# Post-LN attention with routed experts: half of the down weights kept on the chip, and the last batch's row gathers split in two

## The chip, the cores and the metric

The kernel runs on one core of a Trainium2 chip. The metric is the device time of one launch in microseconds (us); lower is better. Before and after compute the same function with the same inputs and outputs. Engines are called as the profile calls them: PE is TensorE (matmuls), PEld its weight loads, DVE is VectorE, ACT is ScalarE, POOL is GpSimd (here above all the issuer of the indirect row gathers), and SP is the queue that issues nearly all other DMAs.

## The reference

The input is `x` of shape (4, 512, 256): four batches of 512 tokens, 256 features.

```python
x = layernorm(x + attention(x))          # 16 heads of 16, causal, ALiBi bias
x = layernorm(x + ffn(x))

def ffn(h):                              # 64 experts, top 8, plus one shared expert
    logits = h @ gate_w.T
    topv, topi = top_k(logits, 8)
    W = scatter(topi, softmax(topv))
    inter = silu(gate_e(h)) * up_e(h)    # each expert e: 256 -> 64
    out = sum_e (inter_e * W[:, e]) @ down_e     # 64 -> 256
    return out + sigmoid(h @ sh_gate1) * shared_expert(h)
```

## The kernel before

All four batches go through two stages that overlap. The first stage is attention, output projection, layer norm and routing. The second is the expert part, and it fills most of the second half of the run.

**Expert part.** The 64 experts of a batch are taken in 16 steps of four (`QUAD`), counted q = 0 to 15; a step of batch b is written b.q below. Each expert has 30 slots (`CELL`) for each 128-token tile, so a step handles up to 120 slots by four experts.

- `gather()` (L995) uses PE to pull the chosen tokens of 16 experts (a group, four steps) into a tile `xt`. It does a group in eight half pieces, each of six short matmuls (L1020), which ACT and DVE copy out of PSUM (L1010).
- `up()` (L1034) first asks for the down weights of the step: a tile `dq` of 128x512 values (256 KB), loaded on SP (L1038), in a ring of four. Then it does 32 matmuls (L1049) and applies the activation, one instruction on ACT (L1057) and two on DVE (L1058, L1059).
- `down()` (L1074) multiplies by `dq` in eight matmuls (L1081). ACT copies the result out of PSUM (L1093), and SP stores it to the DRAM table `rows_out[b]` (L1094), in the order of steps: row = (q, slot, expert).
- `fetch()` (L1156) brings rows back for each tile t of 128 tokens and each of its eight chosen experts k: one indirect DMA on POOL (L1160), 128 rows of 256, into a ring of eight buffers `got` (`RING`). So a batch needs 4 x 8 = 32 gathers, and all four need 128.
- `combine()` (L1167) multiplies the gathered rows by their weight and adds them to `xs[b]` on DVE (L1171). After the last k of certain tiles it runs the second layer norm and stores the output.

**Which rows a gather may need.** Within a token the eight row numbers are sorted, the greatest first. Therefore k = 4 to 7 are the lower four of eight, and where a batch is handled in two halves their gathers are given a table slice that leaves out the last step. Batches 0 to 2 do this: first all (t, k = 4 to 7), then all (t, k = 0 to 3), and row numbers of the first half are clamped below the last step (L876 to L878).

**The last batch.** `LATE = (0, 0, 0, 4)`: the last four steps of batch 3 (3.12 to 3.15) never go through DRAM. Their results stay in SBUF (L1088), weights are spread over the slots by DMA and DVE (`spread_in()` L1102, `weigh()` L1113), and `collect()` (L1125) adds them by 128 matmuls into PSUM (L1135) and four additions of 128x256 (L1143). So for batch 3 the table's last step is 3.11. Before the change this batch is not done in two halves: its 32 gathers go tile by tile, and each may read the whole table, step 3.11 included.

**What sets the order.** Every function above is a generator, and `ORDER` (L37) is a string with one letter for each resumption: p, s, v, o, r for the first stage, h, g, u, d for the expert steps, i for a gather, c for a combine, w, e, k for the late steps, z for the final range check. The string is played once while the program is built, so each engine receives its instructions in that order and runs its own queue strictly in it. In the region that matters later, before the change PE has: all of group 3.3 (steps 3.12 to 3.15) mixed with ups 3.8 and 3.9; then down 3.7, down 3.8, up 3.10, up 3.11, down 3.9, down 3.10, up 3.12, down 3.11, down 3.12, up 3.13 to 3.15 and the collects. The first gather of batch 3 is queued on POOL after the gathers of batch 2.

**Attention's buffers.** In `context()` (L740) a 128x512 tile `avs` with two buffers holds sums on their way to DRAM (L760 to L762); in `output()` (L778) a 128x512 tile `scale`, also with two buffers, holds the normalisation that comes back (L788). `cxT`, 128x2x512, has two buffers (L743). None of them is used any more when batch 3's output projection (L808) has run.

Of the kernel before, what the change touches and what calls it, by code (L numbers as in the profile page):

```python
# [8 lines left out]
FP = mybir.dt.float32  # L9
# [3 lines left out]
ALU = mybir.AluOpType  # L13
AX = mybir.AxisListType

P = 128
HEADS, HD = 16, 16
TOP = 8
# [10 lines left out]
QUAD = 4  # L29
RING = 8  # L30
PRB = (2, 1, 1)
LATE = (0, 0, 0, 4)
# [4 lines left out]
ORDER = (  # L37
    "pppppspppspsppsvvvsppvsvsvsvsvvspsovsvpsvvvspsppopposvvsvsoovsrrrvvsvspsvvvrhrosrrsvvsvrhrsvsrsrprhh"
    "rgvvvspogspprvphphporshvrvvsoorsprrgsvvvgsroghsvrgsrvvrvsrrsvsgvvsorvsrrgvvorsvsrosorsorrrrvvsvsvvvv"
    "tuguugguuggrhglogrgdrruuugrddrruuurrdorlgguuruuggdgrougrudgogrugllrugdudduggruuggrghrhhuuhgdhhdguuuu"  # L40
    "ghddgrrhugudguudrghgriiirgdgiguggruuuiiiuugicigcduigucigdcrgdigcuucgciuugddrczcccgigciiiiricduruuigg"
    "igugrgcguuiggcdgcihhucudhcuuhicddiughuuudcihggiiciugucddgirchhuiguuugdgcgccddggicciciuuucugcgguccgud"
    "guigciiicduccddccgcguugccggguiiguicchccuudugiiidcciigiiiiguucugigdgccuuigigchcidhiucduhhiuducghdchuu"
    "cgguudchcigghcuudigcuiugdgcidccdcigicuuiggcicuiguigiuccgudugggiiucicidcdccdcccruuccgggguuiciigcuwwug"
    "gccdugidgiiicichdgiuccugccggieguccugecuiiiicdiiduuuiucciccdcduiddwciicciiicicicuuiuuucciwccicciccccc"
    "uceecckdiiidkciicdciickicicicckicicckicicicicciiiiiiicickickiiccccccccccckcccz"
)
# [362 lines left out]
def kernel(  # L410
# [23 lines left out]
    nc = tc.nc  # L434
    fast = ctx.enter_context(ExitStack())
    B, S, E = x.shape
    NT = S // P
# [302 lines left out]
    def context():  # L740

        for b in range(B):
            cxT = cxs[b] = mpool.tile([P, KC, S], FP, tag="cxT", name=f"cxT_{b}", bufs=2)  # L743
            for c, par, n in units:
# [12 lines left out]
                if n < len(blocks) - 1:  # L757
                    yield
                    continue
                avs = mpool.tile([P, S], FP, tag="avs", name=f"avs_{b}_{c}_{par}", bufs=2)  # L760
                nc.scalar.copy(avs, av)
# [16 lines left out]
    def output():  # L778

        for b in range(B):  # L780
            scales = []
            for c in range(KC):
                part = slice(HEADS // KC * c, HEADS // KC * (c + 1))
                rs = sums_in[b, c]
                rel = small.tile([P, SPAN], FP, tag="rel", name=f"rel_{b}_{c}")
                nc.vector.reciprocal(rs, rs)
                nc.sync.dma_start(out=turned[b][part].rearrange("h (j i) -> (h j) i", i=SPAN), in_=rs)
                scale = mpool.tile([P, S], FP, tag="scale", name=f"scale_{b}_{c}", bufs=2)  # L788
                for h in range(HEADS // KC):
                    nc.sync.dma_start(  # L790
                        out=scale[HD * h : HD * (h + 1), :],
                        in_=turned[b][part][h : h + 1, :].to_broadcast([HD, S]),
                    )
                scales.append(scale)
                nc.vector.tensor_tensor(rel, rs, least[:, c, :], ALU.mult)
                nc.vector.scalar_tensor_tensor(fine, rs, 1.0 / LIMIT, fine, ALU.is_ge, ALU.mult)
                nc.vector.scalar_tensor_tensor(fine, rel, LIMIT, fine, ALU.is_le, ALU.mult)
                yield
            cxT = cxs[b]
            for c in range(KC):  # L800
                nc.vector.tensor_tensor(cxT[:, c, :], cxT[:, c, :], scales[c], ALU.mult)
            yield
            xb = xs[b]
            for t in range(0, NT, 2):
                po = single(f"po_{b}_{t}").rearrange("p (t e) -> p t e", e=E)
                for u in range(2):
# [10 lines left out]
    def route():  # L817

        for b in range(B):
# [47 lines left out]
            nc.vector.scalar_tensor_tensor(row, place, float(QUAD), number, ALU.mult, ALU.add)  # L867
            nc.vector.tensor_tensor(row, row, chosen, ALU.mult)
            r8 = small.tile([P, NT, TOP], FP, tag="r8", name=f"r8_{b}")
            for t in range(NT):  # L870
# [4 lines left out]
            nc.vector.tensor_scalar(at, near, SOON[b] - 1.0, None, ALU.min)  # L875
            if not LATE[b]:  # L876
                part = slice(TOP // 2, TOP)
                nc.vector.tensor_scalar(at[:, :, part], near[:, :, part], SOON[b] - QUAD * SLOTS - 1.0, None, ALU.min)  # L878
            ats[b] = at
# [27 lines left out]
            if LATE[b]:  # L907
# [5 lines left out]
                nc.vector.reciprocal(total, total)  # L913
                nc.vector.memset(rest[:, :, FIRST[b] :], 0.0)
                yield
# [8 lines left out]
                for t in range(NT):  # L924
                    nc.tensor.transpose(pt[: 2 * EL, t * P : (t + 1) * P], pair[:, t].rearrange("p w e -> p (w e)"), ident)
                flip = rpool.tile([P, TOP, NE], FP, tag="pick", name=f"flip_{b}", bufs=2)
                flip = flip.rearrange("p k e -> p (k e)")
# [67 lines left out]
    def gather():  # L995

        for n, (b, g) in enumerate(groups):
# [7 lines left out]
            for t in range(NT):  # L1005
# [9 lines left out]
                for turn in range(2):  # L1015
# [16 lines left out]
                    yield  # L1032

    def up():  # L1034

        for n, (b, q) in enumerate(steps):
            dq = late["pool"].tile([P, QUAD // 2, E], FP, tag="dq", name=f"dq_{b}_{q}", bufs=4)
            nc.sync.dma_start(out=dq, in_=dp[:, 2 * q : 2 * q + 2, :])  # L1038
            downs[n] = dq
# [85 lines left out]
    def collect():  # L1125

        for b in range(B):
# [3 lines left out]
            for n in range(LATE[b]):  # L1131
# [8 lines left out]
                yield  # L1140
            for t in range(NT):
                part = xs[b][:, t, :]
                nc.vector.tensor_tensor(part, acc[t // 2][:, t % 2, 0:E], part, ALU.add)  # L1143
                yield
# [4 lines left out]
    for b in range(B):  # L1149
        if LATE[b]:  # L1150
            moves += [(b, t, k) for t in range(NT) for k in range(TOP)]
        else:
            moves += [(b, t, k) for t in range(NT) for k in range(HALF, TOP)]
            moves += [(b, t, k) for t in range(NT) for k in range(HALF)]

    def fetch():  # L1156

        for n, (b, t, k) in enumerate(moves):
            g = got[n] = late["pool"].tile([P, E], FP, tag="got", name=f"got_{b}_{t}_{k}", bufs=RING)
            nc.gpsimd.indirect_dma_start(  # L1160
                out=g, out_offset=None, in_=rows_out[b][0 : SOON[b] - (QUAD * SLOTS if not LATE[b] and k >= HALF else 0)],
                in_offset=bass.IndirectOffsetOnAxis(ap=ats[b][:, t, k : k + 1], axis=0),
                bounds_check=None, oob_is_err=True,
            )
            yield

    def combine():  # L1167

        for n, (b, t, k) in enumerate(moves):
# [4 lines left out]
            yield  # L1174
            last = k == (HALF - 1 if not LATE[b] else TOP - 1)
            if b < B - 1 and t % 2 and last:
# [110 lines left out]
```

## Time and profile before

| | |
|---|---|
| median of 3 timed runs | 525.33 us (525.16 to 530.65) |
| the profiled execution, its own time | 479.91 us |
| its span, first to last instruction | 477.4 us |
| mean granted PE clock in it | 0.959 |
| DMA traffic | 82.68 MB, of it 64 loads of `dq` of 256 KB and 60 stores of `rows_out` of 480 KB |
| PE busy in 300 to 400 us | 95.9 of 100 us |
| PE busy in 400 to 440 us | 31.5 of 40 us |
| PE busy in 440 to 478 us | 3.6 of 38 us |
| POOL gathers | 128, mean 980 ns each |

The profiled execution is 45.4 us shorter than the median of the timed runs. The page does not say where the timed runs spend the difference. Durations below are those of the profiled execution.

The page is read from the top: busy shares, then the 40 slices (one is about 12 us), then the chain that ended last. Attention fills the slices up to about 180 us, and then the expert part follows. The last three slices are different from all others: PE has little or nothing left, and POOL and DVE finish.

### The profile page before, as it was taken

The numbers are of one execution on the slowest core, as the hardware profiler recorded it, in microseconds if no ns is written. First come the engines' busy times: TensorE is split into PE (matmuls) and PEld (weight loads), VectorE is DVE, ScalarE is ACT, GpSimd is POOL, SyncE is SP. The second block draws the span as 40 slices with busy tenths as digits, with TensorE's granted clock in tenths as the row PEclk, the third lists the DMA queues.
The fourth block names the chain that finished last, engine by engine and source line by source line (L and its number), as shares of the span: only waits on it lengthen the run. The fifth ranks groups of instructions, "written<-read, shape, count | busy, mean of one in ns | idle before, by whom it ended". The sixth has DMA issues, their size and how long they took to land.

```text
span 477.4 us, 12454 instructions
## 1 busy us (share of the span) xinstructions
PE 423.1 (89%) x4887; PEld 284.3 (60%) x4887; DVE 339.7 (71%) x922; ACT 244.8 (51%) x454; POOL 205.6 (43%) x238
## 2 busy tenths in 40 slices
PE   8999999998999989999999999999999997878100
PEld 3535454453644556876878778777787775765100
DVE  1522326798976888986786798889778898487474
ACT  2658647773578734446646547563566545322000
POOL 6424522253324610310027664266553666457771
PEclk9999999999999999999999999999999999897855
DMA  7900110000000043886868969889899899798342
GB/s 215 405 36 5 28 25 3 24 7 24 3 25 28 8 170 99 260 284 250 240 161 280 284 210 299 267 241 305 267 283 317 255 289 325 231 278 212 105 105 74
DMA packets 37238, 82.68 MB, mean 173 GB/s; under 512 B 8276, under 2 KB 14548, under 8 KB 36148
## 3 DMA queue, kind: packets, MB, share of 16 engines
q1 hardware_dynamic: 30484, 64.51, 43.1%
q0 software_dynamic: 6144, 16.79, 12.1%
q8 instruction: 40, 0.66, 0.6%
q10 hardware_dynamic: 544, 0.52, 0.3%
q14 instruction: 26, 0.21, 0.1%
HBM read 49.88 MB, written 31.92 MB: 171 GB/s over the span
## 4 chain that ended last, share of the span: by engine, by line
PE 68%; DVE 12%; DMA 8%; ACT 4%; issue 3%; POOL 2%; SPq 1%; DVEq 0%; POOLq 0%; ACTq 0%
PE gu L1049 19%; PE y L1081 11%; PE px L1020 9%; PE sT L724 8%; PE av L752 6%; DMA got<-rows_out,at 4%; PE pv L695 3%; PE pq L678 3%; PE pk L678 3%; PE po L808 2%; DMA dq<-in_dp_dram 2%; ACT yq L1093 2%; PE plT L828 2%; DVE x L1171 1%; PE sh L889 1%
## 5 line engine op out<-in xcount | busy, mean ns | idle before, releaser
L1160 POOL DMA_INDIRECT got<-rows_out,at x128 | 125.5, 980 | 128.8 <-DVE x L1171 57.8
L1049 PE MATMUL gu<-xt,gu_sb 128*64 128x120 f32 (+1 forms) x2048 | 118.9, 271 | 1.4 <-DVE ma L1059 1.4
L1049 PEld LDWEIGHTS gu<-xt,gu_sb 128*64 128x64 f32 x2048 | 106.2, 138 | 16.8 <-issue 14.1
L729 ACT ACTIVATE pr<-sT 128x768 f32<-128x768 f32 (+1 forms) x96 | 79.5, 884 | 29.4 <-PE sT L724 29.2
L734 POOL TENSOR_SCALAR_AFFINE_SELECT pr<-pr 128x512 f32<-128x512 f32 x64 | 41.8, 666 | 83.5 <-ACT pr L729 80.7
L1081 PE MATMUL y<-dq,ma 64*120 64x256 f32 (+1 forms) x512 | 68.5, 393 | 8.9 <-DMA dq<-in_dp_dram 5.6
L1093 ACT COPY yq<-y 120x1024 f32<-120x1024 f32 x60 | 59.9, 1012 | 29.4 <-PE y L1081 24.6
L1171 DVE SCALAR_TENSOR_TENSOR x<-got,w,x 128x256 f32<-128x256 f32 x128 | 62.7, 493 | 15.2 <-DMA got<-rows_out,at 13.5
L1081 PEld LDWEIGHTS y<-dq,ma 64*120 64x120 f32 (+1 forms) x512 | 44.5, 182 | 21.4 <-DVE x L1171 4.1
L1057 ACT ACTIVATE ma<-gu 128x240 f32<-128x240 f32 (+1 forms) x64 | 23.7, 371 | 59.9 <-PE gu L1049 51.5
L1010 ACT COPY xt<-px 128x192 f32<-128x192 f32 (+1 forms) x128 | 44.7, 365 | 17.0 <-PE px L1020 13.3
L724 PE MATMUL sT<-qT,kT 32*128 32x256 f32 (+3 forms) x512 | 51.9, 468 | 0.0
L1010 DVE COPY xt<-px 128x480 f32<-128x480 f32 x64 | 41.4, 650 | 14.2 <-ACT xt L1010 13.9
L942 POOL TENSOR_TENSOR pick<-pick,rest 128x512 f32<-128x512 f32 x16 | 21.3, 1334 | 48.2 <-ACT rest L903 25.3
L1020 PE MATMUL px<-hot,xh 64*128 64x288 bf16 x256 | 37.5, 287 | 4.8 <-ACT xt L1010 3.7
L752 PE MATMUL av<-pr,va 128*32 128x128 f32 (+3 forms) x512 | 40.2, 438 | 0.8 <-POOL pr L734 0.8
L1058 DVE SCALAR_TENSOR_TENSOR ma<-ma,gu 128x240 f32<-128x240 f32 (+1 forms) x64 | 25.6, 400 | 18.6 <-ACT ma L1057 18.4
L1020 PE MATMUL px<-hot,xl 64*128 64x288 bf16 x256 | 37.0, 283 | 0.0
L1020 PE MATMUL px<-hot,xm 64*128 64x288 bf16 x256 | 37.0, 282 | 0.0
L724 PEld LDWEIGHTS sT<-qT,kT 32*128 32x128 f32 x512 | 24.4, 183 | 19.7 <-issue 11.5
L752 PEld LDWEIGHTS av<-pr,va 128*32 128x32 f32 x512 | 13.8, 109 | 28.4 <-issue 17.6
L1059 DVE TENSOR_TENSOR ma<-gu,ma 128x240 f32<-128x240 f32 (+1 forms) x64 | 26.1, 408 | 2.2
(148 smaller groups left out, 488.6 us busy)
## 6 DMA issues: line engine op xcount, KB each, us to landing
rows_out<-yq SPq DMA_DIRECT2D x60, 480.0 KB, 5.2
dq<-in_dp_dram SPq DMA_DIRECT2D x64, 256.0 KB, 5.3
gu_sb<-in_gu_dram SPq DMA_DIRECT2D x8, 1024.0 KB, 11.1
scale<-turned SPq DMA_DIRECT2D x64, 32.0 KB, 1.8
got<-rows_out,at POOLq DMA_INDIRECT x128
gu_sb<-spread SPq DMA_DIRECT2D x16, 128.0 KB, 7.3
x<-in_x_dram SPq DMA_DIRECT2D x3, 512.0 KB
out_dram<-x SPq DMA_DIRECT2D x6, 256.0 KB
```

The source lines that it names most:

```text
L678: nc.tensor.matmul(ps, w_sb[n][:, kc, c * P : (c + 1) * P], xT[:, kc, :], start=(kc == 0), stop=(kc == KC - 1),)
L724: nc.tensor.matmul(s_ps[r // 2][:, r % 2, lo : lo + widths[m]], kTs[b][rows, c, kb * P : (kb + 1) * P], qTs[b][rows, c, par, kb * P :], st ...
L729: nc.scalar.activation(pr[:, 2 * i : 2 * i + 2, :], s_ps[i][:, :, : sum(widths)], AF.Exp, scale=1.0 / HD**0.5)
L734: nc.gpsimd.affine_select(out=pr[:, :, lo : lo + P], in_=pr[:, :, lo : lo + P], pattern=[[0, 4], [1, P]], compare_op=ALU.is_ge, fill=0.0, ...
L752: nc.tensor.matmul(av[32 * r : 32 * r + 32, kb * P :], vas[b % 2][:, kb, 8 * c + 2 * r + par, :], pr[:, r, lo : lo + w], start=(kb == 0), ...
L1010: copy(xt[:, kc, :, t * wide + lo : t * wide + hi], ps[:, kc, lo * GROUP : hi * GROUP].rearrange("p (s e) -> p e s", e=GROUP),)
L1020: nc.tensor.matmul(ps[:, kc, first : first + WIDTH * GROUP], parts[b][i][PART * half : PART * half + PART, t, kc * P : (kc + 1) * P], o[PA ...
L1049: nc.tensor.matmul(gu_ps[64 * e : 64 * e + 64, j, which, :], gu_sb[p // GUC][:, p % GUC, kc, which, 64 * e : 64 * e + 64], xt[:, kc, QUAD ...
L1081: nc.tensor.matmul(ys[:, e, j, :], a[64 * e : 64 * e + 64, j, :], dq[64 * e : 64 * e + 64, j, :], start=True, stop=True,)
L1093: nc.scalar.copy(yq.rearrange("s j e h -> s e j h"), ys)
L1160: nc.gpsimd.indirect_dma_start(out=g, out_offset=None, in_=rows_out[b][0 : SOON[b] - (QUAD * SLOTS if not LATE[b] and k >= HALF else 0)], ...
L1171: nc.vector.scalar_tensor_tensor(acc[:, t, :], got.pop(n), w8s[b][:, t, k : k + 1], acc[:, t, :], ALU.mult, ALU.add)
```

## The change

Four edits go together.

1. **Down weights of steps 8 to 15.** They are loaded once, with batch 0, into four tiles of 128x1024 which take over the buffers of `cxT` (two), `scale` and `avs`; the later batches use them from there. Steps 0 to 7 are loaded for each batch as before. To make the buffers large enough, `avs` and `scale` become one tile of 128x2x512 for both halves, with a single buffer each. So 40 loads of `dq` are left of 64.
2. **Two halves for batch 3 as well.** Gathers with k = 4 to 7 come first and read the table without step 3.11; those with k = 0 to 3 follow. For this the row numbers of the late experts are set to zero before the sort, and the weights of late experts are set to zero in `dense`, which takes the place of `rest`.
3. **`collect()`** adds its PSUM result in two instructions of 128x512 in place of four of 128x256.
4. **A new `ORDER`**, from its first 20 letters on. On PE near the end it is now: up 3.8, up 3.9, down 3.7, down 3.8, up 3.10, down 3.9, down 3.10, then group 3.3 with up 3.11 after its third half piece, down 3.11, up 3.12, 3.13, 3.14, down 3.12, up 3.15, down 3.13, down 3.14, collects 0 and 1, down 3.15, collects 2 and 3. On SP the stores of 3.9 and 3.10 are followed by the output store of batch 2's first half, 12 spread loads, the output store of its second half, and then the store of 3.11. On DVE the combines of batch 3's first half stand between the copies of group 3.3 and the activations of 3.11 to 3.15. The range check (z) has moved from the middle of the expert part to the last gathers.

```diff
@@ ORDER
...
@@ context()
-                avs = mpool.tile([P, S], FP, tag="avs", name=f"avs_{b}_{c}_{par}", bufs=2)
+                if par == 0:
+                    both = mpool.tile([P, KC, S], FP, tag="avs", name=f"avs_{b}_{c}")
+                avs = both[:, par, :]
@@ output()
-            scales = []
+            scale = mpool.tile([P, KC, S], FP, tag="scale", name=f"scale_{b}")
...
-                nc.vector.tensor_tensor(cxT[:, c, :], cxT[:, c, :], scales[c], ALU.mult)
+                nc.vector.tensor_tensor(cxT[:, c, :], cxT[:, c, :], scale[:, c, :], ALU.mult)
@@ route()
             nc.vector.tensor_tensor(row, row, chosen, ALU.mult)
+            if LATE[b]:
+                nc.vector.memset(row[:, :, FIRST[b] :], 0.0)
...
-            if not LATE[b]:
-                part = slice(TOP // 2, TOP)
-                nc.vector.tensor_scalar(at[:, :, part], near[:, :, part], SOON[b] - QUAD * SLOTS - 1.0, None, ALU.min)
+            part = slice(TOP // 2, TOP)
+            nc.vector.tensor_scalar(at[:, :, part], near[:, :, part], SOON[b] - QUAD * SLOTS - 1.0, None, ALU.min)
...
-                nc.vector.memset(rest[:, :, FIRST[b] :], 0.0)
...
+                nc.vector.memset(dense[:, :, FIRST[b] :], 0.0)
+                rest = dense
@@ up()
+    beds, stays = {}, {}
+
+    def stay(n):
+        bed, place = divmod(n, 2)
+        if bed not in beds:
+            tag, bufs = (("cxT", 2), ("cxT", 2), ("scale", 1), ("avs", 1))[bed]
+            old = mpool.tile([P, KC, S], FP, tag=tag, name=f"bed{bed}", bufs=bufs)
+            beds[bed] = old.rearrange("p k s -> p (k s)").rearrange("p (i w e) -> p i w e", i=2, w=QUAD // 2)
+        return beds[bed][:, place]
+
...
-            dq = late["pool"].tile([P, QUAD // 2, E], FP, tag="dq", name=f"dq_{b}_{q}", bufs=4)
-            nc.sync.dma_start(out=dq, in_=dp[:, 2 * q : 2 * q + 2, :])
+            if q < NQ // 2:
+                dq = late["pool"].tile([P, QUAD // 2, E], FP, tag="dq", name=f"dq_{b}_{q}", bufs=4)
+            elif b == 0:
+                stays[q] = dq = stay(q - NQ // 2)
+            else:
+                dq = stays[q]
+            if q < NQ // 2 or b == 0:
+                nc.sync.dma_start(out=dq, in_=dp[:, 2 * q : 2 * q + 2, :])
@@ collect()
-            for t in range(NT):
-                part = xs[b][:, t, :]
-                nc.vector.tensor_tensor(part, acc[t // 2][:, t % 2, 0:E], part, ALU.add)
+            for i in range(2):
+                part = xs[b][:, 2 * i : 2 * i + 2, :]
+                nc.vector.tensor_tensor(part, acc[i][:, :, 0:E], part, ALU.add)
                 yield
@@ moves, fetch(), combine()
     for b in range(B):
-        if LATE[b]:
-            moves += [(b, t, k) for t in range(NT) for k in range(TOP)]
-        else:
-            moves += [(b, t, k) for t in range(NT) for k in range(HALF, TOP)]
-            moves += [(b, t, k) for t in range(NT) for k in range(HALF)]
+        moves += [(b, t, k) for t in range(NT) for k in range(HALF, TOP)]
+        moves += [(b, t, k) for t in range(NT) for k in range(HALF)]
...
-                out=g, out_offset=None, in_=rows_out[b][0 : SOON[b] - (QUAD * SLOTS if not LATE[b] and k >= HALF else 0)],
+                out=g, out_offset=None, in_=rows_out[b][0 : SOON[b] - (QUAD * SLOTS if k >= HALF else 0)],
```

More of the change, by code (lines that the diff above doesn't have):

```diff
@@ L37 @@
 ORDER = (
[L38 to L46, printed above, removed]
+    "pppppspppspsppsvvvspspsvvvsvsvvspsvvospsvvvspspopppsvvsvsoovosrrrvvsvsphpsvvvrsrsvorrsvvsrvhsrpsgvvh"
+    "osvhvrsrrpgrospvvrvhsoroossrrrrvhvsvsvvsvvrhsprsorprprgrsrrrpggrvvvsorgvhvsrorsvsvsosrrorvvsvsvvvghg"
+    "vtugrgguuuruoggrrdgguurgldulrrugddggrrouuuuggruuggrdgrugudggluggudrgglughdohhhohuuuddruhuuugddgrguuh"
+    "uudrduhggrggrggrrudiigugrdidrrruchugguugcugugiiciicciiigurdiigdiudugcidrcccciiiciigciugcuricucugiigd"
+    "cicigugggcdcgigcucrugcigdughuhduiihhucuduughhdciuuhdhguuugdcdgcigdggccuiuggcgdihigciciuciuurgcguuggc"
+    "ugucccdduugccdcgguugccuuiiiiiiigdguuccgdgciciciiuicircguddgccuuccgggccgiguighiiiiidcuhhudhcuugcdihii"
+    "cdghciuiuuugugdchuhducgdgccgdgccuugicgggcgcuiuuucccidggiiiiidccuiiucccdgcdcuuggicgcuciiiiiciuuuggcic"
+    "iduggucidcccgccuuddchriiuuciuiiiddcuciccucdcdciiiciciciciccccciwiiwwgciigicgcicciucucigcciiggggcuccc"
+    "duiucuieiccuuccucduiideccdikkcdiwceekiiiiikcciiiicciizccikiicccckccccccccccz"
 )
@@ L787, in output @@
                 nc.sync.dma_start(out=turned[b][part].rearrange("h (j i) -> (h j) i", i=SPAN), in_=rs)
-                scale = mpool.tile([P, S], FP, tag="scale", name=f"scale_{b}_{c}", bufs=2)
                 for h in range(HEADS // KC):
                     nc.sync.dma_start(
-                        out=scale[HD * h : HD * (h + 1), :],
+                        out=scale[HD * h : HD * (h + 1), c, :],
                         in_=turned[b][part][h : h + 1, :].to_broadcast([HD, S]),
                     )
-                scales.append(scale)
                 nc.vector.tensor_tensor(rel, rs, least[:, c, :], ALU.mult)
@@ L1174, in combine @@
             yield
-            last = k == (HALF - 1 if not LATE[b] else TOP - 1)
+            last = k == HALF - 1
             if b < B - 1 and t % 2 and last:
```

## The prediction

> **What bounds the kernel now.** I read the slices, then the chain that ended last, then POOL's and PE's timelines over the last 80 us, then the waits of PE before that.
>
> ```profile
> PE   8999999998999989999999999999999997878100
> PEclk9999999999999999999999999999999999897855
> DMA  7900110000000043886868969889899899798342
> ```
>
> Until slice 34 (about 400 us) PE is full at full clock. Windows give the idle time: 4.1 us of 300 to 400, and over 0 to 400 us I add up 10.3 us. So no edit before 400 us can win more than those 10 us; the matmuls stay the same. After that PE falls away and something else sets the end. The chain names it:
>
> ```profile
> 396.66 1.44 PE gu L1049 x25
> 398.10 9.18 DMA dq<-in_dp_dram
> 407.42 1.61 PE y L1081 x8
> 409.03 4.57 PE gu L1049 x64
> ...
> 429.16 7.31 DMA got<-rows_out,at
> ...
> 465.98 2.98 DMA got<-rows_out,at
> ```
>
> The second line is a down weight load that took 9.18 us; PE stood for its last part. The timeline of PE has "3.67" as idle time there and, at 430.83, another 1.91 us for a `dq`. After 429 us the chain is gathers only. POOL's timeline shows how these run:
>
> ```profile
> 422.12 0.94 POOL L1160 DMA_INDIRECT got<-rows_out,at  x1 [0.31 <-DVE step L622]
> 426.54 0.94 POOL L1160 DMA_INDIRECT got<-rows_out,at  x1 [3.48 <-DMA gu_sb<-spread]
> 427.79 1.07 POOL L1160 DMA_INDIRECT got<-rows_out,at  x1 [0.30 <-DVE x L1171]
> ...
> 464.73 0.95 POOL L1160 DMA_INDIRECT got<-rows_out,at  x1 [0.30 <-DVE x L1171]
> 465.98 1.07 POOL L1160 DMA_INDIRECT got<-rows_out,at  x1 [0.30 <-DVE x L1171]
> ```
>
> From 426.54 to 465.98 are exactly 32 starts: all of batch 3. Their pace is (465.98 - 426.54)/31 = 1.27 us, nearly all POOL's own (0.95 plus 0.30 between). The wait before the first is put down to another DMA, but by the code it is the store of step 3.11: SP's timeline has its issues up to 419.6, so 6.9 us passed until POOL could go. Hence the end is: store of 3.11, then 32 x 1.27 us on POOL, then 11.4 us (465.98 to 477.4). PE ends at 443.6 and has slack.
>
> **The change, part by part.** I count in the profiled execution.
>
> *Loads of `dq`.* 24 of 64 go, 6 MB of 82.7. On the path lie the pause of 3.67 us and what it did to the clock: the 8 matmuls after it took 1.61 us where others take 0.86, and the next 64 took 4.57 where others take 3.43. That is 3.7 + 0.75 + 1.1 = 5.6 us, all before step 3.11 is done. The 1.91 us later lie beside the gathers: nothing. The 40 loads that stay are issued as far ahead as before, about 5 to 8 us of PE work, against 5.3 us to land. Batch 0's loads for steps 10 and 11 now wait on SP for batch 3's output projection, and stores queue behind; down 0.10 follows about 7.7 us of PE work later, so between 0 and 2 us; I take 0.
>
> *Which store starts the gathers.* Before, PE ended down 3.11 at about 418.5. After, only 3.10 is needed, and less stands ahead of it on PE: up 3.12 and down 3.11 (1.92 + 1.06, less overlap 2.9), group 3.3 (eight half pieces at 0.37 plus copies' stalls of 0.4: 3.4) and up 3.11 (1.79), together 8.1 us. Down 3.10 then stands only one down (0.95) behind its own up, where its operand takes ACT 0.37 + DVE 0.40 + 0.41 + 0.1: +0.4. So down 3.10 ends at 418.5 - 5.6 - 8.1 + 0.4 = 405.2; ACT's copy (1.01) ends at 406.3; with the same 6.9 us the first gather starts at T = 413.2. The median of such stores is 5.2 us, which would give 411.5. I take the slower one, since it is this stage's. Lead: 426.5 - 413.2 = 13.3 us.
>
> *Does the train run through?* POOL must be free of batch 2 by T: it ended that at 423.1 before, with 6.0 us lost on a full ring while PE paused, and its second half's first gather now stands two ups earlier. Gather 17 needs step 3.11 at T + 16 x 1.27 = 433.5. DVE decides that. From 403.7 it has activation 3.10 (0.8), 11 combines of batch 2 (11 x 0.49 = 5.4), two layer norms (4.3 each, rows 419.07 to 423.1), a memset and a copy of group 3.3 (0.9): 419.5. Then two combines, activation 3.11 and one copy (2.5): 422. Down 3.11 on PE needs the PSUM buffer this copy frees, so it ends near 423, ACT at 424.1, and the store lands at 431. On SP it stands behind 12 spread loads and an output store that waits for the second layer norm (419.5): passed by then. Slack 2.5 us. Ring: gather 9 (T + 10.2 = 423.4) needs the first combine (420). The table's clamp and the zeroed weights are DVE instructions of 0.2 to 0.5 us in mid-run, and the range check is four small ones between gathers; both stand in DVE's gaps of 1.27 us per gather or beside PE, at nothing.
>
> *The end.* Before, 465.98 to 477.4. After, tile 3's four gathers come last and the layer norm of tiles 0 to 2 stands before their combines on DVE. Gather 28 starts at T + 34.3; landing 3.2, combine 0.5, addition 0.7 (128x512, row L812: 684 ns), layer norm of three tiles 4.6 (459.69 to 464.26), four combines 2.0, then 7.4 as before (470.03 to 477.4): T + 52.7, where before it was 50.9. So +1.8.
>
> *PE's clock in the tail.* PE will now stand between ups and downs that wait for DVE, so the clock matters. The trace has both speeds:
>
> ```profile
> 426.92 2.01 PE L1135 MATMUL acc<-gu_sb,gu_sb 32*128 32x256 f32 x32
> 435.11 3.73 PE L1135 MATMUL acc<-gu_sb,gu_sb 32*128 32x256 f32 x32
> 439.83 3.74 PE L1135 MATMUL acc<-gu_sb,gu_sb 32*128 32x256 f32 x64
> ```
>
> The middle row is after idle time (granted clock 0.50 in 432 to 436). The Trainium skill, "TensorE: Matmul & The Clock Gate", section "Part 1: The HAM clock gate", says the clock halves after an idle window of about 3.4 us and needs as long busy to return. By that rule all PE work after down 3.11 (four ups, four downs, four collects, about 19.5 us at full clock) could take twice as long: collects would end near 423 + 39 = 462, past gather 24 (446), and the end would slip by some 12 us, eating the gain. The trace's own mix is milder: 408.95 to 443.57, pauses of some 5 us included, held 25 us of such work, a factor of 1.2 without the pauses. That gives 423 + 23 = 446 plus waits on DVE, just in time. I take the trace, and cost 0, with up to +12.
>
> *The order before 400 us.* Its stalls are what they are in the new string. Two pieces of one group tile that follow each other directly cost 0.41 us; outside group 3.3 there are eight such pairs before and eight after. Downs at most three PE pieces behind their own up were two, and are seven. One costs 0 to 0.9 us (PE waited 0.9 us once for L1059). Bounds: -7 (all idle time of 180 to 400 gone, with less DMA) and +6; I take +1. In attention, `avs` has one buffer per pair, so the copy of the next pair waits for the store and the DVE reader of the last: copies of different pairs are at least 5.7 us apart, a store's issue follows within 1 us and lands in some 2; nothing.
>
> **Sum.** -13.3 + 1.8 + 1 = -10.5: the profiled execution would go from 479.9 to 469.4. The timed median is 45.4 us above that execution and I cannot say why. If it is a fixed part, 10.5 comes off; if PE is slower there, the moved PE work counts for more and the `dq` pause, with DMA less pressed, for less. I keep 10.5: 525.3 - 10.5 = 514.8.
>
> **The rivals.**
>
> *Small gain.* The pause at 404 us is one execution's chance, or gone where PE is slower: 5.6 us less. Or DVE reaches the second layer norm later than 422: beyond 2.5 us each us is passed on through SP to the store of 3.11 and gathers 17 to 32. For it: one pause of that size in the whole trace, and a slack smaller than my errors. Against: DMA is at 1.03 in 396 to 404. Time: 525.3 - 10.5 + 5 to + 12, 520 to 527.
>
> *The order makes it slower.* The seven downs close behind their up wait not for an idle DVE but behind what it has queued, a layer norm (3.4 to 4.6) or a `hot` (0.75). At 0.9 each it is 6 us; from 1.5 us each (10.5 in all) the gain is gone, from 2.3 (16) it is slower by over 1%. Pauses above 3 us also cost clock as at 408. Against it: DVE is 83% busy in 300 to 400 us, yet PE waited for an activation just once in 180 to 400. Time 531 to 538.
>
> *It does less than it says.* The first half might still wait for the whole table. Batches 0 to 2 already gather this way with the same slice, so this is unlikely; then the last gathers start at 431 and all is as before, plus 4 us: within the slower case.
>
> *More gain.* With 6 MB less, most PE stalls before 400 go too: 500 to 509.
>
> **How the numbers follow.** Forecast (510 to 519): 0.57. More: 0.08. Small gain: 0.19, nearly all within 1%. Slower, both ways: 0.16. A measurement of this kernel tells about 1% (5.3 us) from no change. Faster by more: 0.64; within: 0.20; slower: 0.16. The range is 506 to 529: it leaves out most of the slower case and part of the large gain.
>
> **What would show it.** First gather of batch 3 near 413 with 32 starts at 1.27 us; no PE wait for `dq` of step 8 or later; the store of 3.11 landed before gather 17; the last layer norm starting 5 to 6 us after the last gather. I am wrong if PE's idle time before 400 us grows past 20 us, if POOL pauses between gathers 16 and 17, or if the last addition waits for the collects.

## The result, and the profile after

The changed kernel took 555.66 us (median of 4 runs, 552.97 to 558.86), where the kernel before took 526.93 (525.16 to 530.65) beside it: 1.054 times as long, with an interval of 1.045 to 1.062. The prediction was 514.8, with a range of 506 to 529.

These are the slices of the changed kernel (13.8 us each). Each digit is the busy share in tenths, PEclk the granted clock.

```profile
span 553.7 us, 12391 instructions
...
PE   8999999999999989996876899777987766648660
...
PEclk9999999999999999997887999898999989667775
```

Until slice 18 (about 249 us) PE is as full as before. Then slices of 6 to 8 stand between full ones, and the clock gives way (a granted 0.90 in 245 to 345 us), all through the expert part and not only at the end. The first gather of rows starts at 245.9 us. Here is the changed kernel's PE timeline over the first train of gathers (gathers that follow each other without a pause; start, duration, engine, line, operation; in brackets the idle time before it, and what ended it), and below it POOL's and ACT's.

```profile
248.31 1.86 PE L1069 MATMUL gu<-xt,gu_sb 128*64 128x120 f32 x32
...
250.36 0.29 PE L1022 MATMUL px<-hot,xl 64*128 64x288 bf16 x2
250.48 0.28 PE L1022 MATMUL px<-hot,xh 64*128 64x288 bf16 x2
250.60 0.28 PE L1022 MATMUL px<-hot,xm 64*128 64x288 bf16 x2
251.80 0.31 PE L1022 MATMUL px<-hot,xl 64*128 64x288 bf16 x2 [0.91 <-issue]
252.52 0.26 PE L1069 MATMUL gu<-xt,gu_sb 128*64 128x120 f32 x1 [0.41 <-issue]
253.23 0.32 PE L1069 MATMUL gu<-xt,gu_sb 128*64 128x120 f32 x2 [0.44 <-issue]
254.64 0.43 PE L1069 MATMUL gu<-xt,gu_sb 128*64 128x120 f32 x4 [1.09 <-issue]
256.08 0.46 PE L1069 MATMUL gu<-xt,gu_sb 128*64 128x120 f32 x3 [1.00 <-issue]
```

```profile
248.64 0.95 POOL L1177 DMA_INDIRECT got<-rows_out,at  x1 [0.30 <-issue]
249.90 0.95 POOL L1177 DMA_INDIRECT got<-rows_out,at  x1 [0.30 <-issue]
251.15 0.95 POOL L1177 DMA_INDIRECT got<-rows_out,at  x1 [0.30 <-issue]
...
256.16 0.95 POOL L1177 DMA_INDIRECT got<-rows_out,at  x1 [0.30 <-issue]
```

```profile
259.01 0.37 ACT L1077 ACTIVATE ma<-gu 128x240 f32<-128x240 f32 x1 [8.89 <-remote]
```

PE waits for nothing that the profile shows ("issue"): a few matmuls, a pause of about 0.3 to 1.1 us, a few matmuls. It begins some 5 us after the train's first gather and lasts until the train is over. ACT is late too: PE ended the up of the first line at 250.17, and the activation that needs it began 8.8 us later, after the train. The recorded profile of the kernel before has almost none of it: its up matmuls had 1.4 us of idle time ahead of them, all waits for DVE. The groups show how much it came to (busy time, mean ns of one, idle time before and what ended most of it), first those of the recorded profile of the kernel before, then those of the changed kernel:

```profile
L1049 PE MATMUL gu<-xt,gu_sb 128*64 128x120 f32 (+1 forms) x2048 | 118.9, 271 | 1.4 <-DVE ma L1059 1.4
...
L1057 ACT ACTIVATE ma<-gu 128x240 f32<-128x240 f32 (+1 forms) x64 | 23.7, 371 | 59.9 <-PE gu L1049 51.5
```

```profile
L1177 POOL DMA_INDIRECT got<-rows_out,at x128 | 125.7, 982 | 194.2 <-DVE x L1188 101.6
L1069 PE MATMUL gu<-xt,gu_sb 128*64 128x120 f32 (+1 forms) x2048 | 139.5, 286 | 24.7 <-issue 23.4
...
L1077 ACT ACTIVATE ma<-gu 128x240 f32<-128x240 f32 (+1 forms) x64 | 23.8, 372 | 129.3 <-remote 57.8
```

The gathers themselves take POOL as long as before (982 against 980 ns each). PE has 23.4 us of unexplained pauses in this one group, and ACT 57.8 us of idle time ("remote": ended by a signal for which the profile finds no instruction that had just finished). None of the edits adds a wait of either kind.

### The profile page after: what moved, and what is told of

Read it like the earlier page. It is cut to its first block, busy times and chain, and to the rows that moved or that the text cites. A ratio compares the mean times of both kernels' runs of the same rounds, so it can differ in the third digit from the quotient of the medians.

```text
span 553.7 us, 12391 instructions
## 1 busy us (share of the span) xinstructions
PE 464.3 (84%) x4887; PEld 307.2 (55%) x4887; DVE 339.5 (61%) x922; ACT 243.5 (44%) x454; POOL 207.4 (37%) x238
## 3 DMA queue, kind: packets, MB, share of 16 engines
q0 software_dynamic: 6144, 16.79, 10.2%
## 5 line engine op out<-in xcount | busy, mean ns | idle before, releaser
L1069 PE MATMUL gu<-xt,gu_sb 128*64 128x120 f32 (+1 forms) x2048 | 139.5, 286 | 24.7 <-issue 23.4
L1069 PEld LDWEIGHTS gu<-xt,gu_sb 128*64 128x64 f32 x2048 | 119.2, 147 | 48.8 <-issue 46.1
L1077 ACT ACTIVATE ma<-gu 128x240 f32<-128x240 f32 (+1 forms) x64 | 23.8, 372 | 129.3 <-remote 57.8
L1022 PE MATMUL px<-hot,xh 64*128 64x288 bf16 x256 | 40.3, 304 | 18.3 <-ACT xt L1012 15.0
L1101 PE MATMUL y<-bed,ma 64*120 64x256 f32 (+1 forms) x256 | 38.5, 426 | 11.3 <-ACT yq L1113 5.6
L1101 PE MATMUL y<-dq,ma 64*120 64x256 f32 x256 | 36.6, 404 | 6.2 <-issue 2.4
L1022 PE MATMUL px<-hot,xl 64*128 64x288 bf16 x256 | 40.0, 301 | 0.9 <-issue 0.9
L1022 PE MATMUL px<-hot,xm 64*128 64x288 bf16 x256 | 40.2, 302 | 0.0
L724 PEld LDWEIGHTS sT<-qT,kT 32*128 32x128 f32 x512 | 24.5, 183 | 21.1 <-issue 11.0
L1022 PEld LDWEIGHTS <-xh 64*128 64x128 bf16 x256 | 15.3, 97 | 37.1 <-issue 33.5
L1101 PEld LDWEIGHTS y<-bed,ma 64*120 64x120 f32 (+1 forms) x256 | 24.3, 196 | 19.6 <-issue 8.7
L944 POOL TENSOR_TENSOR pick<-pick,rest 128x512 f32<-128x512 f32 x12 | 16.6, 1386 | 39.1 <-ACT rest L904 25.7
```

The costliest lines, as they stand in the source:

```text
L724: nc.tensor.matmul(s_ps[r // 2][:, r % 2, lo : lo + widths[m]], kTs[b][rows, c, kb * P : (kb + 1) * P], qTs[b][rows, c, par, kb * P :], st ...
L1022: nc.tensor.matmul(ps[:, kc, first : first + WIDTH * GROUP], parts[b][i][PART * half : PART * half + PART, t, kc * P : (kc + 1) * P], o[PA ...
L1069: nc.tensor.matmul(gu_ps[64 * e : 64 * e + 64, j, which, :], gu_sb[p // GUC][:, p % GUC, kc, which, 64 * e : 64 * e + 64], xt[:, kc, QUAD ...
L1101: nc.tensor.matmul(ys[:, e, j, :], a[64 * e : 64 * e + 64, j, :], dq[64 * e : 64 * e + 64, j, :], start=True, stop=True,)
```

## The experiments

**One part at a time.** The first four runs, all on chip 12 (the chip of the first comparison and of the recorded execution isn't on record), ask whether the edits or the new order make the loss. First the kernel before, once more.

> The unchanged kernel, to have its profile from the same session as the changed one's. Theory G (PE's issue slows down wherever row gathers run beside it; the changed kernel only has more of that): this trace, too, shows PE stops put down to issue inside stretches with gathers from about 245 us on, the span is near 523 to 528 and not 477, and PE's clock is below 0.959. Theory O (the new order's own dependencies make the stops): no such stops, span near 477, though then the timed 527 stays unexplained.

It took 522.96 us beside 526.2. Its span is 521.1 us, and it has pauses of the same kind, so the recorded execution of 479.9 us was not like the runs that were timed.

All edits of the change, with the order of before:

```diff
 ORDER = (
-    (the new string)
+    (the string of before, without its last two k)
 )
```

> All edits of the change, but with the order string of before (less two letters for the two additions that fall away). Theory O or G (the order is what costs): the time is that of before or up to 8 us better, 517 to 530. Theory B (the kept down weights in the attention's buffers cost): still slower, 545 to 560.

521.8 us, 0.993 of the kernel before (0.987 to 0.999). The edits by themselves cost nothing here; the loss comes with the new order.

The changed kernel with `dq` loaded at every step:

```diff
-            if q < NQ // 2:
-                dq = late["pool"].tile(...)
...
-            if q < NQ // 2 or b == 0:
-                nc.sync.dma_start(out=dq, in_=dp[:, 2 * q : 2 * q + 2, :])
+            dq = late["pool"].tile([P, QUAD // 2, E], FP, tag="dq", name=f"dq_{b}_{q}", bufs=4)
+            nc.sync.dma_start(out=dq, in_=dp[:, 2 * q : 2 * q + 2, :])
```

> The changed kernel with the down weights loaded for every step again, so the new order and the split batch 3 alone. Theory O or G: as slow as the changed kernel or slower, 550 to 570, since 6 MB of loads come back. Theory B: back to before, 515 to 530.

560.11 us, 1.066 (1.059 to 1.072), 4.5 us more than the changed kernel's 555.66 of the first comparison. The new order is slower with or without them.

The kernel before with the kept weights alone (edit 1 of the change, order of before):

> The kernel before with the kept down weights alone (old order, batch 3 in one part). Theory O or G: 0 to 8 us faster than before, 519 to 528. Theory B: slower, 540 to 560.

523.68 us, 0.994 (0.986 to 1.002): not to be told from no change here.

**Without the gathers.** Both kernels with the 128 gathers left out:

```diff
-            g = got[n] = late["pool"].tile(...)
-            nc.gpsimd.indirect_dma_start(...)
+            got[n] = still
```

> The kernel before with all 128 row gathers left out; the combines run on a constant tile of zeros, so the experts' rows are left out of the output. Theory G (gathers issued back to back slow PE's instructions and hand-offs): PE's stops put down to issue vanish, PE ends near 440 us instead of 499, the span is 440 to 460. Theory O (stops come from the order's own dependencies): PE still ends at 480 or later.

> The same with the changed kernel. Theory G: the new order costs nothing without gathers, so the span is within 8 us of the kernel before without gathers (435 to 460). Theory O: it stays 25 us or more longer than that one.

459.58 and 461.16 us, one run each (chip 12; the kernel before took 522.36 beside them). Without gathers the whole change, new order included, thus costs 1.6 us, far from the 29 of the first comparison. Set against the times with gathers, these cost 522.4 - 459.6 = 63 us in the kernel before and 555.7 - 461.2 = 94 us in the changed one, whose 555.7 is from the first comparison.

**Shorter trains.** On this chip gathers of the kernel before follow each other in trains of up to 24 (457.7 to 488.6 us). PE stood for 21.0 of those 30.9 us; in the 33 trains of one to three gathers before PE's end it stood for 1.7 of 53.7 us. Of the 21.0, 16.52 are one pause that is put down to "issue". The lines of ACT beside it tell more:

```profile
461.72 1.14 PE L1081 MATMUL y<-dq,ma 64*128 64x256 f32 x8 [1.90 <-issue]
479.38 2.08 PE L1081 MATMUL y<-dq,ma 64*128 64x256 f32 x8 [16.52 <-issue]
...
478.32 1.01 ACT L1088 COPY gu_sb<-y 128x1024 f32<-128x1024 f32 x1 [20.01 <-remote]
```

The same three in the recorded execution:

```profile
430.83 1.16 PE L1081 MATMUL y<-dq,ma 64*128 64x256 f32 x8 [1.91 <-DMA dq<-in_dp_dram]
433.10 2.08 PE L1081 MATMUL y<-dq,ma 64*128 64x256 f32 x8 [1.10 <-ACT gu_sb L1088]
...
432.03 1.01 ACT L1088 COPY gu_sb<-y 128x1024 f32<-128x1024 f32 x1 [4.62 <-PE y L1081]
```

In both the second down starts within 0.06 us of the end of ACT's copy of the first. But the copy began 0.04 us after the first down in the recorded execution, and 15.5 us after it here. So this long pause is a late hand-off from PE to ACT, not PE's own.

The changed kernel has more long trains: nine of five or more gathers, where the kernel before has five. With `RING = 3`, and each gather held back in the order behind the combine that frees its buffer, trains become short:

```diff
-RING = 8
+RING = 3
 ORDER = (
-    (each i where it was)
+    (each i not before the combine of the gather three earlier)
 )
```

> The changed kernel with a ring of 3 gather buffers instead of 8, gathers that would run further ahead queued behind the combine that frees their buffer. Bursts of POOL are then short. Theory G: PE ends earlier than the changed kernel's 535 by 15 to 40 us, time 515 to 540. Theory O: no gain, and DVE waits longer for rows, 555 to 580.

> The kernel before with the same ring of 3. Theory G: PE ends before 499 by 5 to 25 us except where the tail is bound by the gathers, time 505 to 525. Theory O: slower, 530 to 545.

The changed kernel took 546.38 us, the kernel before 532.2, both outside what the theory of long trains expected (515 to 540, 505 to 525). Against the kernel before run beside them they are 1.048 (1.036 to 1.060) and 1.021 (1.012 to 1.030). The first lies within the interval of the change without short trains (1.045 to 1.062), so that short trains help the changed kernel is not shown; in the kernel before they cost some 2%. From the first gather until PE's end PE stood 30.8 us within gathers and 36.6 us outside them in the changed kernel with three buffers, and 40.6 and 24.5 us in the changed kernel of the first comparison. Shorter trains moved the pauses and did not take them away.

**What about a gather costs.** In place of the indirect DMA a plain one of the same size from the same queue:

```diff
-            nc.gpsimd.indirect_dma_start(
-                out=g, out_offset=None, in_=rows_out[b][0 : SOON[b] - ...],
-                in_offset=bass.IndirectOffsetOnAxis(ap=ats[b][:, t, k : k + 1], axis=0),
-                bounds_check=None, oob_is_err=True,
-            )
+            nc.gpsimd.dma_start(out=g, in_=rows_out[b][(last 128 rows of that slice)])
```

> The changed kernel, in which each of the 128 gathers is replaced by a plain transfer of the same size from POOL's queue into the same buffer: it reads the last 128 rows of the same slice of the table, one per partition, in place of the rows that the indices name. The waits, the ring of five and the places in the order stay; the output is not the reference's. Without any gathers the changed kernel took 461 us, with them 556. Theory A (what costs is the gather's address-driven form: rows named one by one from a tile of indices): close to the kernel without gathers, 460 to 485. Theory B (the 128 transfers' traffic beside weights and stores): as with gathers, 540 to 560. Theory C (POOL's work of issuing a DMA in software, whatever its form): as with gathers, 540 to 560, while the same transfers from SP's queue are cheap.

> The same replacement in the kernel before (without gathers 460, with them 522 to 526). Theory A: 460 to 485, and within 10 us of the changed kernel so altered. Theories B and C: 515 to 530, 25 to 35 below the changed kernel so altered.

> The changed kernel with the same plain transfers issued from SP's queue; SP then stands for their waits, so loads behind them can come later, which may cost some 10 to 20 us by itself. Theory B (traffic): 540 or more. Theories A and C (form, or POOL's issuing): 460 to 490. Together with the same transfers from POOL's queue this separates C (POOL slow, SP fast) from A (both fast).

(The ring has eight buffers; "five" is a slip.) They took 466.27, 473.24 (two runs, 469.31 and 477.16) and 475.96 us, which fits theory A. But these three ran on chip 3, and there the kernel before took 482.38 us (479.0 to 482.63), not 526. So these runs told less of the gathers than of where they ran: the kernel before, unchanged, is some 43 us faster there, and near the recorded execution of 479.91. So the changed kernel itself had to be run where the kernel before takes 482.

> The changed kernel unchanged, beside the kernel before. In the last session the kernel before took 479 to 483 us on another chip (number 3), where every earlier session (chip 12) had 520 to 530; so chips differ by some 45 us on this kernel, and the recorded profile of 479.9 us fits the faster kind. Theory D (the order is no worse by itself; what costs is how a chip of the slower kind carries gathers beside the other engines): on a chip where the kernel before takes about 480, the changed kernel takes 465 to 475, near the sum of the prediction (469.4); on one where it takes about 526, again 553 to 559. Theory E (the new order costs 5 per cent wherever it runs): about 1.05 times the kernel before on either chip, so 503 to 510 where that takes 480.

> All edits of the change with the order of before (without its last two pieces). Theory D: where the kernel before takes 480, within 2 per cent of it and slower than the changed kernel by 5 to 15 us; where it takes 526, 519 to 524 again. Theory E: within 1 per cent of the kernel before on either chip, and 20 us or more below the changed kernel.

> The changed kernel with plain transfers from POOL's queue in place of the gathers (fixed rows of the table in place of the named ones), as on chip 3, where it took 466. On a chip where the kernel before takes 526, the address-driven form as the cost means 460 to 480; POOL's issuing of any DMA as the cost means 530 or more. On a chip where it takes 480: 464 to 469 again.

> The kernel before with the same replacement (469 to 477 on chip 3). On a chip where the kernel before takes 526: 465 to 485 if the address-driven form is the cost, 505 or more if any DMA from POOL's queue is.

These four fell on chip 9. The kernel before took 482.87 us (480.82 to 483.55), the changed kernel 469.62 (467.98 to 471.99): 0.974, with an interval of 0.969 to 0.978. **The same change is 2.7% faster here and 5.4% slower in the first comparison.** All edits with the old order took 475.14 (0.986, 0.982 to 0.990), and the plain transfers 466.74 and 472.49. Theory E, that the order costs 5% everywhere, falls; D's number for such a chip (465 to 475) holds. By the difference between these two, the order alone gains 5.5 us here.

The slices and groups of the changed kernel on chip 9 (a slice is 11.7 us):

```profile
span 468.1 us, 12391 instructions
...
PE   9999999989999999999999999999999899837920
...
PEclk9999999999999999999999999999999999986975
...
L1177 POOL DMA_INDIRECT got<-rows_out,at x128 | 126.4, 988 | 117.9 <-DMA rows_out<-yq 43.3
L1069 PE MATMUL gu<-xt,gu_sb 128*64 128x120 f32 (+1 forms) x2048 | 119.1, 271 | 1.8 <-DVE ma L1079 1.2
...
L1077 ACT ACTIVATE ma<-gu 128x240 f32<-128x240 f32 (+1 forms) x64 | 23.7, 370 | 58.9 <-PE gu L1069 56.8
```

It is the same program with the same number of instructions, and a gather takes 988 ns where it took 982. But PE has 1.8 us of pauses in its up matmuls in place of 24.7, and ACT's idle time is the ordinary wait for PE. The matmuls differ as well: in the first comparison PE ended 87.7 us later than here (535.4 against 447.6), and 40.1 us of that are longer busy time (464.3 against 424.2 us) under a lower granted clock (0.90 against 1.00 in 245 to 345 us, 286 against 271 ns for an up matmul). During the same first train, PE on chip 9 ran on (its timeline; POOL's gathers here start at 246.93, and then every 1.25 us):

```profile
249.31 1.86 PE L1069 MATMUL gu<-xt,gu_sb 128*64 128x120 f32 x32
251.10 0.30 PE L1022 MATMUL px<-hot,xh 64*128 64x288 bf16 x2
251.23 0.29 PE L1022 MATMUL px<-hot,xm 64*128 64x288 bf16 x2
251.36 0.29 PE L1022 MATMUL px<-hot,xl 64*128 64x288 bf16 x2
251.48 0.29 PE L1022 MATMUL px<-hot,xh 64*128 64x288 bf16 x2
...
251.21 0.37 ACT L1077 ACTIVATE ma<-gu 128x240 f32<-128x240 f32 x1
```

ACT began the activation of the first line's up 0.04 us after it, where it took 8.8 us in the first comparison.

In this first train (13 gathers, 16.4 us) PE stood for 0.5 us in all, where it stood for 4.1 us of 11.2 in the first comparison. In a later train of 24 (381.2 to 411.8 us) it was 2.5 us. The trains are longer here than there, and do little harm.

What of the gather costs where it does cost was still open. The plain transfers were run again:

> The changed kernel with plain transfers from POOL's queue in place of the gathers (fixed rows of the table in place of the named ones), sent a third time for a chip of the slower kind. Where the kernel before takes about 526: 460 to 480 if the address-driven form is what costs there, 530 or more if any DMA issued by POOL does. Where it takes about 482: 464 to 469, as on chips 3 and 9.

This fell on chip 1, where the kernel before took 523.84 us. The changed kernel with plain transfers took 464.55, as on chips 3 and 9 (0.886, 0.873 to 0.899). Its traffic is that of the gathers: the profile counts 6144 packets and 16.79 MB on POOL's queue (q0) in both. So POOL's queue, the traffic and the waits on the table are not what costs; the address-driven transfer is. Last, its form without the scattered rows:

```diff
+    line = const.tile([P, 1], I32, name="line")
+    nc.gpsimd.iota(line, pattern=[[0, 1]], base=0, channel_multiplier=1)
-                in_offset=bass.IndirectOffsetOnAxis(ap=ats[b][:, t, k : k + 1], axis=0),
+                in_offset=bass.IndirectOffsetOnAxis(ap=line, axis=0),
```

> The changed kernel with its gathers kept as address-driven DMAs, but with one constant column of indices: partition p always reads row p of the table, so the 128 rows of a gather are distinct and lie one behind the other, as in the plain transfers. The rows are not the chosen ones. On a chip where the kernel before takes about 526: 545 to 560 if it is the form of the instruction that costs (the address list read by POOL, or the packets made from it), 460 to 490 if it is the scattered rows. On a chip where it takes about 482: 464 to 472, and it tells nothing of this.

Chip 5, the kernel before at 525.94: 552.62 us (1.048, 1.028 to 1.069). Its groups, the first fence, stand as in the first comparison; those of the plain transfers on chip 1, the second, stand as on chip 9:

```profile
L1179 POOL DMA_INDIRECT got<-rows_out,line x128 | 125.2, 978 | 189.3 <-DVE x L1190 105.7
L1071 PE MATMUL gu<-xt,gu_sb 128*64 128x120 f32 (+1 forms) x2048 | 138.8, 286 | 23.9 <-issue 22.8
...
L1079 ACT ACTIVATE ma<-gu 128x240 f32<-128x240 f32 (+1 forms) x64 | 23.8, 372 | 118.9 <-remote 54.8
```

```profile
L1177 POOL DMA_DIRECT2D got<-rows_out x128 | 68.4, 539 | 160.7 <-DVE x L1184 86.0
L1069 PE MATMUL gu<-xt,gu_sb 128*64 128x120 f32 (+1 forms) x2048 | 117.6, 270 | 0.9 <-DVE ma L1079 0.9
```

Whether the rows lie scattered or in order thus makes no difference that these runs show. What costs is the form of the instruction; with it goes the longer time that POOL spends on each (978 against 539 ns), and the two are not told apart.

## Why the prediction was right and wrong

**The step that failed** is the last of the sum: "The timed median is 45.4 us above that execution and I cannot say why. If it is a fixed part, 10.5 comes off ... I keep 10.5: 525.3 - 10.5 = 514.8." The 45.4 us were no fixed part. They were a cost of the gathers beside PE and ACT where the timed runs were made, nearly absent from the profiled execution, and the change to the order made just this larger. Chip 12 isn't slower in itself: without gathers the kernel before took 459.6 us there. The start of the last matmul of a batch's last down (of step 11 in batch 3), by the traces, shows where the time goes:

| | first gather | down 0.15 | down 1.15 | down 2.15 | down 3.11 |
|---|---|---|---|---|---|
| before, recorded execution | 246.2 | 245.2 | 305.5 | 364.6 | 418.1 |
| before, chip 12 | 246.4 | 245.5 | 317.7 | 389.0 | 449.1 |
| after, chip 9 | 246.9 | 245.2 | 306.7 | 372.0 | 425.3 |
| after, first comparison | 245.9 | 244.2 | 332.3 | 416.8 | 488.9 |

Up to the first gather the rows agree within 1.3 us. From there the kernel before loses 31 us by step 3.11 (449.1 - 418.1), and the changed one 64 us (488.9 - 425.3). The prediction named the gap, wrote down "if PE is slower there, the moved PE work counts for more", and then gave it no price. Its own sign of being wrong came true in the first comparison: before 400 us PE stood for 33.9 us (20 was the limit), 28.0 of them after 245 us; in the recorded execution it was 12.0.

**On the machine that the profile showed, the sum held.** It made 469.4 us of 479.9; chip 9 gave 469.62, with 482.87 before. That the two agree within 0.2 us is in part luck: against the kernel before on chip 9 the gain is 13.3 us and not 10.5, and against the recorded execution the span is 9.3 us shorter (468.1 against 477.4). Its steps, against the changed kernel's trace of chip 9:

```profile
410.88 0.94 POOL L1177 DMA_INDIRECT got<-rows_out,at  x1 [0.30 <-DVE x L1188]
414.84 0.94 POOL L1177 DMA_INDIRECT got<-rows_out,at  x1 [3.01 <-DMA rows_out<-yq]
...
433.67 0.95 POOL L1177 DMA_INDIRECT got<-rows_out,at  x1 [0.30 <-DVE marks L1137]
434.92 0.95 POOL L1177 DMA_INDIRECT got<-rows_out,at  x1 [0.30 <-DVE gu_sb L1140]
...
454.84 0.95 POOL L1177 DMA_INDIRECT got<-rows_out,at  x1 [0.30 <-DVE st L607]
```

- *Which store starts the gathers.* Predicted T = 413.2, measured 414.84, after a wait of 3.01 us for a store of the table. Down 3.10 was to end at 405.2 and ended at 405.86.
- *The train runs through.* Gather 17 was to start at 433.5 and did at 434.92, 0.30 us after the gather before it: no pause between 16 and 17, and one of 0.85 us after gather 17. DVE ended the second layer norm at 421.7 (predicted 419.5) and the copy that down 3.11 needs at 423.8 (predicted 422). Down 3.11 ended at 426.0 where 423 was predicted; with gather 17 later too, some 0.9 us of the slack of 2.5 us was left, by an estimate from these times and the landing time that the prediction took.
- *The end.* T + 52.7 predicted; 468.1 - 414.84 = 53.3.
- *Loads of `dq`.* Predicted 5.6 us before step 3.11. With the old order and all edits on chip 9, the last matmul of down 3.11 started at 413.0, where the recorded execution of before had it at 418.1: 5.1 us, from one execution each.
- *The order before 400 us.* Predicted +1 between -7 and +6. No run isolates this term; with it down 3.10 was to end at 406.2, and on chip 9 it ended at 405.86. So the terms up to there were right as a sum, and one by one that isn't shown. The term was of no help in the first comparison: it had no place for what the order does to the gathers' neighbours.
- *PE's clock in the tail.* Taken at 0, with up to 12 us. On chip 9:

```profile
404.73 1.13 PE L1101 MATMUL y<-bed,ma 64*120 64x256 f32 x8 [0.39 <-DVE ma L1079]
...
416.57 0.42 PE L1022 MATMUL px<-hot,xh 64*128 64x288 bf16 x2 [4.57 <-DVE xt L1012]
...
423.90 2.06 PE L1101 MATMUL y<-bed,ma 64*120 64x256 f32 x8 [5.12 <-DVE xt L1012]
```

After pauses of 4.57 and 5.12 us the eight matmuls of down 3.11 took 2.06 us, where those of 3.10 took 1.13; the granted clock was 0.51 in 416.5 to 424 us and 1.00 in 405 to 412. This agrees with the rule of the Trainium skill ("TensorE: Matmul & The Clock Gate", "Part 1: The HAM clock gate"), by which the clock halves after an idle window of about 3.4 us. The collects ended at 447.5 (predicted 446), 7.3 us before the last gather starts. So the slow clock came, but not the 12 us.

**The rivals.** "The order makes it slower" had the sign of the first comparison, but neither its size (531 to 538) nor its mechanism: downs close behind their ups would cost without gathers too, and there the two kernels are 1.6 us apart. "Small gain" and "more gain" fit neither kind of chip. "It does less than it says" is ruled out: on chip 9 batch 3's first gather started at 414.84, before down 3.11 had run.

**What stays open.** Stops of PE and ACT beside address-driven gathers are in the traces of chips 12 and 5 and of the first comparison, and hardly in that of chip 9; for chips 1 and 3 only times tell of them. The chip of the first comparison isn't on record, and the unaltered changed kernel was not timed again on a chip of the slower kind. The groups of runs came in the order of chips 12, 12, 3, 9, 1, 5: a steady drift is ruled out, but no chip was seen in both kinds, so that it is the chip, and not a spell of time that took in the two groups on 3 and 9, is likely and not shown. The instruction loads that the profile counts don't differ (40 packets, 0.66 MB on queue q8, in the first comparison and on chip 9). What differs, and through what path a gather holds back PE's issue and the hand-offs, no run shows. The traces' records of the counters by which engines signal each other may be a lead: 644 changes are recorded for DVE's counter on chip 12 where 773 of its instructions raise it (kernel before), but 753 for 751 there without gathers and 794 for 793 in the changed kernel on chip 9. Signals that came late and several at once would look like this; lost records would too. Nor is it shown why the new order loses more.

Of the versions timed on both kinds of chip, all edits with the old order was slower on neither: 0.986 of the kernel before on chip 9, and 0.993 on chip 12.

## What to carry to other kernels

If the profiled execution and the timed runs are far apart (here 480 and 525 us), that gap is the first thing to explain: the profile may then describe other conditions than those that are timed, and a sum made on it is a forecast for the former. Write a price for the gap under each cause that you can think of, and see whether the change feeds one of them. Where a program issues many indirect gathers beside dense PE work, compare a version with plain transfers of the same size, and time both on more than one chip before you tune the order around them.

## What the runs showed of the hardware

- The same program, the kernel before, took 522 to 526 us (medians) on chips 1, 5 and 12 and 482 to 483 on chips 3 and 9. Without gathers it took 459.6 on chip 12.
- An indirect gather of 128 rows took POOL 0.98 to 0.99 us on both kinds; a plain transfer of the same size 0.54 us. On chip 1 the plain ones left the other engines alone (464.55 us for the whole kernel); on chip 5 indirect ones with rows in order did not (552.62).
- The stops don't come with more DMA traffic: the DMA share was 0.57 in 245 to 345 us of the changed kernel in the first comparison, where chip 9 had 0.77. The stops slow the kernel, and so lower that share themselves.
- Beside gathers on the slower kind not only PE's matmuls stop. Work that ACT does on PE's results began late: 8.8 us after PE had ended in the first comparison (0.04 us on chip 9), and 15.5 us on chip 12 (0.04 us in the recorded execution).
- The granted clock can halve without one long pause of PE. In the first comparison PE worked for 1.07 us of the 3.4 from 253.0 to 256.4 us, with no pause over 1.1 us; from 256.4 to 263.2 us the granted clock was 0.50.
